# Linear attention and a 2:4-sparse feed-forward: the layer input of four tile pairs transposed by VectorE and HBM instead of TensorE

## The chip, the core and the metric

The kernel runs on one core of a Trainium2 chip, in float32 throughout. The metric is device time in microseconds. Five engines work side by side, each through its own queue of instructions in a fixed order: PE (TensorE, with its weight loads shown apart as PEld), DVE (VectorE), ACT (ScalarE), POOL (GpSimd) and SP, which here only issues DMAs. An instruction waits at the head of its queue for what it needs, and everything behind it waits too.

## What is computed

```python
# x: [2, 1024, 512]; 16 query heads, 4 key/value heads of 128
x = x + layernorm(attention(layernorm(x)))
x = x + layernorm(ffn(layernorm(x)))

# attention: q, k, v = x @ W.T; rope on q and k; elu + 1 on both;
#   state += k v^T and z += k along the sequence, out = (q state) / (q z + 1e-6); out @ Wo.T
# ffn: h = silu(x @ w_gate) * (x @ w_up); of each 4 neighbours the 2 largest are kept; h @ w_down
```

The change touches one thing in this: how the first `layernorm(x)` of half of the sequence gets from rows (tokens on partitions) into columns (model dimension on partitions), which is the form in which TensorE takes it as a factor.

## The kernel before

**Steps.** The attention part runs in 16 steps: eight chunks of 128 tokens (of both batch entries, a "tile pair") for the first half of the heads, and then the same eight for the second half (`STEPS = 2 * NC`). In step n TensorE makes the key/value and query products of tile pair n+1, the scores and attention of n, and the output products of n-1, woven by hand in the loop over `n`. Products are made by a seven-product scheme with sums of quarters, `chain` (L509). Its `snapshot` copies of a running bank, "u copies" below (L528, ACT), are waited for by the chain's next product into that bank.

**Input of a step.** In step n the pair n+2 is prepared. `step_normalize` (L672) takes statistics, root and normalization on DVE and ACT and leaves the result in `x`. Its root on ACT waits in the plan for the signal `("root", n)`, given after a step's fourth product. `step_input` (L680) is called late in the step, once for each of the two batch entries: four TensorE transposes into a PSUM bank (`transposed`, whose instructions carry L498), ACT copies out of it (L691, L697) and, for the second entry, four subtractions on DVE (L700, L704). This gives `xf`, seven factors of 128 x 256. They are stored to HBM (L707), and steps 8 to 15 read them from there (`step_input_again`, L713). In steps 6 and 7 the pairs n+2 are already these stored ones.

**A transpose without TensorE.** Queries and attention outputs go another way, `moved` (L625): DVE transposes 32x32 blocks within each partition group (L630) into one of three `blocks` buffers, one DMA stores the 256 KB to HBM (L636), and four DMAs of 64 KB read them back with blocks exchanged (L643).

**The order.** Nothing but TensorE's order is written by hand. The class `Plan` plays the engines through while the program is being built: each piece of work is a generator that yields (engine, length, rank) or a name to wait for, and of the work that is ready the lowest rank goes first. The rank is 1 unless given. What comes out is the fixed order of each queue. Lengths and transfer times in it are estimates, and a float that is yielded alone is a pause. Weights are prepared beside all this by `prepare_all`: loads on SP (L425), sums on POOL (L449), stores (L451), in parts that TensorE's progress sets free.

Other names used below: `features` (rope and elu+1 of queries and keys, with ACT lines 779 and 781), `attend` (the division is L972), `o_sums` (L1038, sums for the output products), `finish` (from step 8 on, layer norm of the attention output), `load` (of `x` at L311).

Of the kernel before, what the change touches and what calls it, by code (L numbers as in the profile page):

```python
# [10 lines left out]
F32 = mybir.dt.float32  # L11
BF16 = mybir.dt.bfloat16
AF = mybir.ActivationFunctionType
ALU = mybir.AluOpType
PSUM = bass.MemoryType.PSUM

P = 128
B, S, DM = 2, 1024, 512
# [3 lines left out]
NIC = DM // P  # L22
NC = S // P
# [88 lines left out]
def kernel(  # L112
# [16 lines left out]
    nc = tc.nc  # L129
# [3 lines left out]
    dram = ctx.enter_context(tc.tile_pool(name="dram", bufs=1, space=bass.MemoryType.DRAM))  # L133
# [9 lines left out]
        out=causal,  # L143
        in_=causal,
# [16 lines left out]
    xf_dram = [dram.tile([P, 7, 2, P], F32, name=f"xf{c}") for c in range(NC)]  # L161

    qb_dram, ob_dram = (
        [[dram.tile([P, 4 * P], F32, name=f"{of}{k}{i}") for i in range(4)] for k in range(2)]
        for of in ("qb", "ob")
    )

    fb_dram = [dram.tile([P, 4 * P], F32, name=f"fb{tt}") for tt in range(4)]
    y_dram = [dram.tile([P, B, DM], F32, name=f"y{c}") for c in range(NC)]
    x2_dram = [dram.tile([P, B, DM], F32, name=f"x2_{c}") for c in range(NC)]  # L170

# [113 lines left out]
    def left(name, bufs, **more):  # L285
        return actx.enter_context(
            tc.tile_pool(name=name, bufs=bufs, reuse_waits="tile", **more)
        )
# [9 lines left out]
    qp = left("a_q", 2)  # L298
# [7 lines left out]
    ln = right("a_ln", 2)  # L306
# [52 lines left out]
    xt, rope_sb = {}, {}  # L359
# [9 lines left out]
    root = const.tile([P, 1], F32, name="root")  # L369
# [85 lines left out]
    plan = Plan()  # L455
# [17 lines left out]
    uses = {}  # L473
# [3 lines left out]
    def ring(name, bufs):  # L477

        k = uses.get(name, 0)
        uses[name] = k + 1  # L480
        return [(name, k - bufs)] if k >= bufs else [], (name, k)
# [126 lines left out]
    def all_of(count, name):  # L608


        def done():
            nonlocal count
            count -= 1
            if count == 0:
                plan.signal(name)

        return done
# [4 lines left out]

    def moved(src, through, new, name, *names):  # L625


        yield "dve", 0.8
        t = qp.tile([P, 4, 4, 32], F32, tag="blocks", name="blocks", bufs=3)
        nc.vector.transpose(  # L630
            out=t.rearrange("p b i r -> p i b r"),
            in_=src.rearrange("p i (b d) -> p i b d", d=32),
        )
        yield 0.2
        yield "sp", 0.44
        nc.sync.dma_start(out=through, in_=t.rearrange("p b i r -> p (b i r)"))  # L636
        yield plan.transfer(256)
        for n in names:
            yield n
        for b in range(4):  # L640
            yield "sp", 0.44
            t = t if b else new()
            nc.sync.dma_start(  # L643
                out=t[b * 32 : (b + 1) * 32],
                in_=through.rearrange("(u d) (b e) -> b d u e", u=4, b=4)[b],
            )
            landing = plan.transfer(64)
        yield landing + 1.5
        plan.signal(name)
# [20 lines left out]
    xf = {}  # L670

    def step_normalize(n, root=None, rank=1):  # L672
        yield "x", n
        scales = yield from layernorm_pair([xt[n][:, b, :] for b in range(B)], B, "a", root, rank)
        for b in range(B):
            yield "dve", 0.56, rank
            normalize(xt[n][:, b, :], xt[n][:, b, :], *scales[b])
            plan.signal(("xn", n, b))

    def step_input(n, b, kind):  # L680

        if b == 0:
            xf[n] = ln.tile([P, 7, 2, P], F32, tag="xf", name="xf")
        t = xf[n]
        pt, name = transposed(
            xt[n][:, b, :].rearrange("p (c d) -> p c d", c=NIC), kind, ("xn", n, b)
        )

        def first():
            yield "act", 0.65, 0  # L690
            nc.scalar.copy(t[:, 0:2].rearrange("p q k d -> p (q k) d"), pt)  # L691
            plan.signal(name)
            plan.signal(("xf0", n))

        def second():
            yield "act", 0.4, 0
            nc.scalar.copy(t[:, 2], pt[:, 2:4, :])  # L697
            yield "xf0", n
            yield "dve", 0.45, 0
            nc.vector.tensor_tensor(t[:, 3], pt[:, 0:2, :], t[:, 0], ALU.subtract)  # L700
            plan.signal(name)
            for to, i0, i1 in ((4, 2, 3), (5, 4, 0), (6, 1, 4)):
                yield "dve", 0.45, 0
                nc.vector.tensor_tensor(t[:, to], t[:, i0], t[:, i1], ALU.subtract)  # L704
            plan.signal(("xf", n))
            yield "sp", 0.44, 2
            nc.sync.dma_start(out=xf_dram[n], in_=t)  # L707
            plan.transfer(896)
            plan.signal(("xf stored", n))

        plan.spawn((first, second)[b]())

    def step_input_again(n):  # L713
        yield "out", n - 2, 0
# [75 lines left out]
    kf, kT, v1, qT = {}, {}, {}, {}  # L790
# [73 lines left out]
    def q_products(n):  # L864
        def place():
            return rawp.tile([P, REP, HD], F32, tag="raw", name="qraw", bufs=5)

        def feature(i, done=None):
            def new():
                qT[n, i] = qp.tile([P, 4, P], F32, tag="qT", name="qT", bufs=4)  # L870
                return qT[n, i]

            def go(src):
                f = yield from features(src, n, done, None, int(n + i > 0))
                plan.signal(("features", n, i))
                if (n, i) in BY_PE:
                    first_q[n, i] = f
                    return
                yield from moved(
                    f, qb_dram[n % 2][i], new, ("qT", n, i), *([("out", n - 1, i)] if n else [])  # L880
                )

            return go

        def q21(b, name):
            yield from feature(2, name)(b)

        return chain(
            ("q", n),
            [P, REP, HD],  # L890
            1.72,
            project(weights[n // NC][1], n),
            lambda i: [("xf", n), ("w", n // NC, 1, i)],
            (qp, "keep512", 2),
            (place, feature(0)),
            (place, feature(3)),
            (place, feature(1)),
            q21,
        )
# [138 lines left out]
    def o_sums(n):  # L1038
        for i in (3, 0, 1, 2):
            yield "of", n, i  # L1040
        if n > 0:
            yield "o", n - 1, 4
        engine = "pool" if n + 1 < STEPS else "dve"

        def t3():
            yield engine, 1.3 if engine == "pool" else 0.75
            eng = nc.gpsimd if engine == "pool" else nc.vector
            eng.tensor_tensor(factor(n, 6 - 1, 1), of[n, 4], of[n, 0], ALU.subtract)
            plan.signal(("of", n, 5))

        yield "dve", 0.8
        nc.vector.tensor_tensor(of[n, 3], of[n, 3], of[n, 0], ALU.subtract)
        plan.signal(("of", n, 3, "sum"))
        yield "dve", 0.8
        nc.vector.tensor_tensor(factor(n, 4, 1), of[n, 2], of[n, 3], ALU.subtract)
        plan.signal(("of", n, 4))
        plan.spawn(t3())
        yield "dve", 0.8
        nc.vector.tensor_tensor(factor(n, 6, 1), of[n, 1], of[n, 4], ALU.subtract)
        plan.signal(("of", n, 6))  # L1060
# [125 lines left out]
    def run(g, times):  # L1186
        for _ in range(times):
            next(g, None)
# [520 lines left out]
    with tc.manual_schedule(engines={E.PE, E.Pool, E.SP, E.DVE, E.Activation}):  # L1709
# [66 lines left out]
        for n in range(STEPS):  # L1776
# [19 lines left out]
                plan.spawn(load(n + 3, "x"))  # L1796
            if n + 2 < STEPS:
                if n + 2 < NC:
                    plan.spawn(step_normalize(n + 2, ("root", n)))
                else:  # L1800
                    plan.spawn(step_input_again(n + 2))
            if n + 2 == NC:
# [45 lines left out]
            if n == 0:  # L1848
                q_transposed(0, 2)
                outputs(1)  # L1850
                run(kvp, 1)
                run(qpr, 1)
                q_transposed(0, 3)
                run(kvp, 1)
                step_input(2, 0, "a")
                outputs(2)
                step_input(2, 1, "a")
                run(qpr, 1)
                outputs(3)
            else:  # L1860
                outputs(1)
                run(qpr, 1)
                run(kvp, 1)
                run(qpr, 1)
                run(kvp, 1)
                run(opr, 2)
                outputs(2)
                if n + 2 < NC:
                    step_input(n + 2, 0, "a")
                run(opr, 2)  # L1870
            if n + 2 == STEPS:
                plan.need(("prepared",), *(("features", n + 1, i) for i in range(4)))
# [2 lines left out]
            if n > 0:  # L1875
                k_transposed(n + 1)
                run(opr, 1)
                if n + 2 < NC:
                    step_input(n + 2, 1, "a")
                outputs(3)  # L1880


# [114 lines left out]
```

## Time and profile before

| what | value |
|---|---|
| median of 3 runs | 1293.47 us (1291.8 to 1295.14) |
| the profiled run | 1293.64 us |
| its span on the core | 1291.9 us |
| four TensorE transposes of `x`, start to start | 0.43 us |
| TensorE transposes of `x` (L498) | 64 |
| DVE block transpose 128x512 (L630) | 0.66 to 0.715 us |
| ACT table load | 1.28 us |
| blocks read back (L643), issue to landing | 2.3 us median |

The span is measured inside the run, which is 1.7 us longer. In all views times are microseconds from the span's start unless ns is named. A row of the timeline has start, length, engine, line, operation, result <- operands, sizes and how many instructions in a row it merges; a bracket at the end is idle time before it and what ended it. A line of a source view has the operation and its count, then the shortest, median and longest duration in ns.

### The profile page before, as it was taken

What the parts mean: (1) busy time and instruction counts of PE and PEld (TensorE: products, weight loads), DVE (VectorE), ACT (ScalarE), POOL (GpSimd) and SP (SyncE); (2) the same over time, 40 slices, a digit from 0 to 9 for tenths busy, and PEclk for the clock granted to TensorE, in tenths of its full rate; (3) what the DMA queues carried; (4) which work ended last, traced back from release to release, by engine and by line L of the source; (5) the groups of instructions that cost most, each with busy time, mean ns of one, the idle gap of its engine ahead of it and who ended that gap; (6) DMA issues with size and microseconds to landing.
All of it is one profiled execution on the core that took longest, in us unless ns stands there. A gap on an engine that the chain in (4) does not pass through costs nothing. (4 is left out here: it accounts for less than half of the span.)

```text
span 1291.9 us, 17317 instructions
## 1 busy us (share of the span) xinstructions
PE 1265.8 (98%) x5868; PEld 1016.8 (79%) x5868; DVE 865.6 (67%) x1519; ACT 455.4 (35%) x905; POOL 340.8 (26%) x261
## 2 busy tenths in 40 slices
PE   7899999999999999999999999999999999999997
PEld 4567777777777777777788887888888888888886
DVE  6987877786666786678764487416981687426763
ACT  3644454444334344434443332113220333023211
POOL 4634442432232454455421101001100110110010
PEclk9999999999999999999999999999999999999999
DMA  7376668659757876676484498367547756465312
GB/s 249 118 244 199 199 231 278 206 194 312 221 195 210 289 228 230 221 236 204 160 249 155 136 265 235 99 199 217 154 123 228 236 155 196 148 189 174 108 44 87
DMA packets 280151, 252.57 MB, mean 196 GB/s; under 512 B 19200, under 2 KB 239104, under 8 KB 277376
## 3 DMA queue, kind: packets, MB, share of 16 engines
q1 hardware_dynamic: 278832, 249.64, 61.9%
q10 hardware_dynamic: 1232, 1.84, 0.4%
q8 instruction: 47, 0.77, 0.2%
q14 instruction: 40, 0.33, 0.1%
HBM read 179.83 MB, written 71.57 MB: 195 GB/s over the span
## 5 line engine op out<-in xcount | busy, mean ns | idle before, releaser
L528 ACT COPY u<-cb 128x512 f32<-128x512 f32 (+1 forms) x252 | 126.4, 503 | 492.5 <-PE cb L250 189.9
L736 PE MATMUL cb<-wq,xf 128*128 128x512 f32 x256 | 120.4, 593 | 1.3 <-ACT u L528 1.3
L1078 PE MATMUL cb<-wo,of 128*128 128x256 f32 x512 | 121.2, 380 | 0.0
L250 PE MATMUL cb<-fxnT,wgu 128*128 128x256 f32 x512 | 117.3, 379 | 2.4 <-issue 1.2
L250 PE MATMUL cb<-fxt,wgu 128*128 128x256 f32 x512 | 117.1, 380 | 1.4 <-ACT u L528 1.4
L776 POOL TENSOR_TENSOR qraw<-qraw,r 128x512 f32<-128x512 f32 x48 | 61.7, 1285 | 201.5 <-DVE qraw L767 174.9
L1078 PEld LDWEIGHTS cb<-wo,of 128*128 128x128 f32 x512 | 95.7, 190 | 23.1 <-issue 11.6
L972 ACT ACTIVATE o<-nm,den 128x128 f32<-128x128 f32 x256 | 73.8, 370 | 109.0 <-DVE state L995 84.2
L250 PEld LDWEIGHTS cb<-fxnT,wgu 128*128 128x128 f32 x512 | 97.1, 190 | 16.1 <-issue 3.1
L250 PEld LDWEIGHTS cb<-fxt,wgu 128*128 128x128 f32 x512 | 97.2, 190 | 15.3 <-ACT u L528 2.2
L1507 POOL TENSOR_TENSOR h<-h 128x512 f32<-128x512 f32 x16 | 26.1, 1629 | 286.9 <-DVE ht L1504 185.5
L539 DVE TENSOR_TENSOR y<-u,ce 128x256 f32<-128x256 f32 (+1 forms) x42 | 18.9, 452 | 117.3 <-ACT u L528 57.3
L449 POOL TENSOR_TENSOR wraw<-wraw 128x512 f32<-128x512 f32 x68 | 96.7, 1422 | 3.0 <-DMA of<-ob 0.4
L955 PE MATMUL nm<-v,am 128*128 128x129 f32 x512 | 96.1, 277 | 1.0 <-ACT o L972 1.0
L954 PE MATMUL nm<-state,qT 128*128 128x129 f32 x448 | 87.6, 278 | 0.0
L736 PEld LDWEIGHTS cb<-wq,xf 128*128 128x128 f32 x256 | 48.3, 190 | 47.7 <-issue 44.5
L955 PEld LDWEIGHTS nm<-v,am 128*128 128x128 f32 x512 | 77.1, 194 | 2.0 <-ACT o L972 1.8
L736 PEld LDWEIGHTS cb<-wkv,xf 128*128 128x128 f32 x256 | 49.1, 192 | 32.9 <-issue 27.3
L954 PEld LDWEIGHTS nm<-state,qT 128*128 128x128 f32 x448 | 72.5, 194 | 2.5
L736 PE MATMUL cb<-wkv,xf 128*128 128x256 f32 x256 | 66.8, 384 | 0.0
L910 PE MATMUL sc<-qT,kT 128*128 128x512 f32 x128 | 65.5, 593 | 0.0
L1078 PE MATMUL ce<-wo,of 128*128 128x256 f32 x256 | 60.5, 379 | 0.0
(172 smaller groups left out, 2458.1 us busy)
## 6 DMA issues: line engine op xcount, KB each, us to landing
wgu<-gs SPq DMA_DIRECT2D x64, 256.0 KB, 3.6
wgu<-us SPq DMA_DIRECT2D x64, 256.0 KB, 3.0
wd<-d_dram SPq DMA_DIRECT2D x32, 512.0 KB, 5.1
qb<-blocks SPq DMA_DIRECT2D x59, 256.0 KB, 2.3
qT<-qb SPq DMA_DIRECT2D x236, 64.0 KB, 2.3
ob<-blocks SPq DMA_DIRECT2D x58, 256.0 KB, 2.5
of<-ob SPq DMA_DIRECT2D x232, 64.0 KB, 2.3
xf<-xf SPq DMA_DIRECT2D x16, 896.0 KB, 4.7
```

Source lines behind the costliest of these rows:

```text
L250: nc.tensor.matmul(bank[:, j, :].rearrange("p (w t) -> p w t", t=32), w[:, k, j, :], xf[xi][:, k], start=(start and j == 0 and k == 0), st ...
L449: nc.gpsimd.tensor_tensor(to, i0, i1, op)
L528: nc.scalar.copy(kept[i], b)
L539: nc.vector.tensor_tensor(dst[:, rows], kept[i][:, rows], b, ALU.add)
L736: nc.tensor.matmul(bank.rearrange("p h d -> p (h d)"), xf[n][:, xi, k, :], w[wi][:, k, :], start=(start and k == 0), stop=(k == 1), skip_g ...
L776: nc.gpsimd.tensor_tensor(u, u, r, ALU.add)
L910: nc.tensor.matmul(sc.rearrange("p u h t -> p (u h t)"), kT[n][:, 2 * b + j, :], qT[n, i].rearrange("p u e -> p (u e)"), start=True, stop= ...
L954: nc.tensor.matmul(dst, q[:, u, :], state[b, j], start=True, stop=False)
L955: nc.tensor.matmul(dst, a[:, u, :], v, start=(c == 0), stop=True)
L972: nc.scalar.activation(t[:, u, :], nmv[:, u // 2, u % 2, 0:HD], AF.Copy, scale=den[:, u // 2, u % 2 : u % 2 + 1],)
L1078: nc.tensor.matmul(bank.rearrange("p h d -> p (h d)"), of[n, xi][:, k, :], weights[gp][2][wi][:, k, :], start=(start and k == 0), stop=(k ...
L1507: nc.gpsimd.tensor_tensor(b12, b22, b12, ALU.subtract)
```

## The change

Pairs 4 to 7 (prepared in steps 2 to 5) no longer call `step_input`. A new function, `step_input_moved`, is started at the beginning of their step: both entries pass through `moved`, with the last four sevenths of the `xf` tile as block buffers and the tile `x` itself as the place to read back to. After a pause of 5.0 in the plan ACT copies the factors from SBUF, and DVE makes the four subtractions from SBUF. Pairs 0 to 3 are transposed as before.

With it go three smaller edits: the root in `step_normalize` waits for no signal from step 1 on; `moved` waits in the plan until one of the three block buffers is free; and two output sums get rank 0 instead of 1.

```diff
@@ moved
-    def moved(src, through, new, name, *names):
-        yield "dve", 0.8
-        t = qp.tile([P, 4, 4, 32], F32, tag="blocks", name="blocks", bufs=3)
+    def moved(src, through, new, name, *names, blocks=None, rank=1):
+        k = -1
+        while not blocks and k < uses.get("blocks", 0) - 3:
+            k = uses["blocks"] - 3
+            yield "blocks", k
+        yield "dve", 0.8, rank
+        if not blocks:
+            block = ring("blocks", 3)[1]
+        t = blocks or qp.tile([P, 4, 4, 32], F32, tag="blocks", name="blocks", bufs=3)
...
         yield plan.transfer(256)
+        if not blocks:
+            plan.signal(block)
@@ new
+    def step_input_moved(n):
+        t = ln.tile([P, 7, 2, P], F32, tag="xf", name="xf")
+        xf[n] = t
+        both = all_of(2, ("xf0", n))
+
+        def tile_in(b):
+            yield "xn", n, b
+            x_ = xt[n][:, b, :]
+            to = x_.rearrange("p (u i r) -> p u (i r)", u=4, r=32)
+            yield from moved(
+                x_.rearrange("p (c d) -> p c d", c=NIC),
+                xb_dram[n % 2][b],
+                lambda: to,
+                ("xm", n, b),
+                blocks=t[:, 3 + 2 * b : 5 + 2 * b].rearrange(
+                    "p q k (i r) -> p (q k) i r", r=32
+                ),
+            )
+            yield 5.0
+            v = x_.rearrange("p (u i r) -> p i u r", u=4, r=32)
+            if b == 0:
+                yield "act", 0.65
+                nc.scalar.copy(t[:, 0:2].rearrange("p q k (u r) -> p (q k) u r", r=32), v)
+            else:
+                yield "act", 0.4
+                nc.scalar.copy(t[:, 2].rearrange("p k (u r) -> p k u r", r=32), v[:, 2:4])
+            both()
+            if b == 1:
+                yield "xf0", n
+                yield "dve", 0.45
+                nc.vector.tensor_tensor(
+                    t[:, 3].rearrange("p k (u r) -> p k u r", r=32),
+                    v[:, 0:2],
+                    t[:, 0].rearrange("p k (u r) -> p k u r", r=32),
+                    ALU.subtract,
+                )
+                for to_, i0, i1 in ((4, 2, 3), (5, 4, 0), (6, 1, 4)):
+                    yield "dve", 0.45
+                    nc.vector.tensor_tensor(t[:, to_], t[:, i0], t[:, i1], ALU.subtract)
+                plan.signal(("xf", n))
+                yield "sp", 0.44, 2
+                nc.sync.dma_start(out=xf_dram[n], in_=t)
...
+        for b in range(B):
+            plan.spawn(tile_in(b))
@@ o_sums, twice
-        yield "dve", 0.8
+        yield "dve", 0.8, 0
@@ loop over steps
-                    plan.spawn(step_normalize(n + 2, ("root", n)))
+                    plan.spawn(step_normalize(n + 2, None if n > 0 else ("root", n)))
+                    if n > 1:
+                        step_input_moved(n + 2)
...
-                if n + 2 < NC:
-                    step_input(n + 2, 0, "a")
+                if n == 1:
+                    step_input(3, 0, "a")
...
-                if n + 2 < NC:
-                    step_input(n + 2, 1, "a")
+                if n == 1:
+                    step_input(3, 1, "a")
```

More of the change, by code (lines that the diff above doesn't have):

```diff
@@ L168 @@
     fb_dram = [dram.tile([P, 4 * P], F32, name=f"fb{tt}") for tt in range(4)]
+    xb_dram = [[dram.tile([P, 4 * P], F32, name=f"xb{k}{b}") for b in range(B)] for k in range(2)]
     y_dram = [dram.tile([P, B, DM], F32, name=f"y{c}") for c in range(NC)]
@@ L711, in step_input @@
         plan.spawn((first, second)[b]())
+    def step_input_moved(n):
[39 more added lines that the diff above has]
+                nc.sync.dma_start(out=xf_dram[n], in_=t)
+                plan.transfer(896)
+                plan.signal(("xf stored", n))
+        for b in range(B):
+            plan.spawn(tile_in(b))
     def step_input_again(n):
@@ L879, in go @@
                 yield from moved(
-                    f, qb_dram[n % 2][i], new, ("qT", n, i), *([("out", n - 1, i)] if n else [])
+                    f,
+                    qb_dram[n % 2][i],
+                    new,
+                    ("qT", n, i),
+                    *([("out", n - 1, i)] if n else []),
+                    rank=1,
                 )
@@ L1049, in t3 @@
             plan.signal(("of", n, 5))
-        yield "dve", 0.8
+        yield "dve", 0.8, 0
         nc.vector.tensor_tensor(of[n, 3], of[n, 3], of[n, 0], ALU.subtract)
         plan.signal(("of", n, 3, "sum"))
-        yield "dve", 0.8
+        yield "dve", 0.8, 0
         nc.vector.tensor_tensor(factor(n, 4, 1), of[n, 2], of[n, 3], ALU.subtract)
```

## The prediction

> **What bounds the kernel now.** I read the page's first two parts, then a table of windows cut at the step borders, then TensorE's timeline, and last the waits. The page's chain of waits does not help: it goes back 2 us from the last output and stops.
>
> ```profile
> span 1291.9 us, 17317 instructions
> ...
> PE 1265.8 (98%) x5868; PEld 1016.8 (79%) x5868; DVE 865.6 (67%) x1519; ACT 455.4 (35%) x905; POOL 340.8 (26%) x261
> ...
> PE   7899999999999999999999999999999999999997
> ```
>
> TensorE is busy for 98% of the span, so only its own work and its few gaps can move the end. The next view cuts the attention part where a step's first query product starts (steps 2 to 6). Columns: window, its length, busy time of each engine, granted clock, DMA share, GB/s.
>
> ```profile
> 114.76:157.70 42.94, 42.94 (x206) 32.03 (x204) 34.04 (x62) 19.40 (x43) 20.22 (x15) 1.00 0.73 235
> 157.70:200.65 42.95, 42.95 (x206) 31.95 (x205) 32.45 (x63) 19.29 (x43) 17.69 (x13) 1.00 0.72 238
> 200.65:243.83 43.18, 43.17 (x205) 32.05 (x204) 33.79 (x63) 19.20 (x43) 16.33 (x13) 1.00 0.65 207
> 243.83:286.77 42.94, 42.94 (x205) 32.03 (x204) 33.61 (x58) 19.53 (x43) 16.76 (x13) 1.00 0.68 229
> 286.77:328.83 42.06, 42.06 (x197) 31.25 (x196) 25.72 (x51) 15.91 (x38) 8.91 (x7) 1.00 0.90 282
> ```
>
> The first four rows are the steps whose input (tile pairs 4 to 7) the change reroutes. TensorE has no gap in them, while DVE, ACT and POOL have 9 to 26 us to spare. The fifth row is nearly the after state: step 6 has the same products and attention, but its input comes ready from HBM. It has 8 matmuls fewer and is 0.88 us shorter. The timeline shows the pieces:
>
> ```profile
> 187.82 0.60 PE L498 MATMUL ca<-ident,x 128*128 128x128 f32 x4
> 188.25 1.89 PE L1078 MATMUL cb<-wo,of 128*128 128x256 f32 x8
> ...
> 193.87 0.61 PE L498 MATMUL ca<-ident,x 128*128 128x128 f32 x4
> ```
>
> Start to start, a group of four transposes holds TensorE for 0.43 us.
>
> **What the change removes.** Eight such groups, two in each of steps 2 to 5: 8 x 0.44 = 3.5 us. By whole steps it is 0.88 + 0.89 + 1.12 + 0.88 = 3.77 us, but 0.24 of step 4's 1.12 is a gap near 235 us, at a product after the key transposes; I don't count on it. **Sum: -3.5 us.** No part was hidden, since the removed instructions stood in a row without gaps.
>
> The skill speaks against this change: "VectorE: DVE Perf Modes", "Rules for kernel authors", says to transpose 128x128 on TensorE if PSUM will do. By it the detour loses, since DVE needs 0.70 us (rows at L630, 0.66 to 0.715) plus two transfers for what TensorE does in 0.43 us. The trace decides for the engine that is full: 0.43 us on the path against 0.70 us on an engine with 9 us free per step. The same page ("The three transpose paths") warns that a plain DMA which transposes by strides is 19 times slower than the crossbar; 19 times its 1309 ns gives an estimate of 25 us per 128x128 block, which would be late in every step. But the nearest row, the same reads for queries and outputs, shows runs of 512 bytes and a short landing:
>
> ```profile
> L643 SPq DMA_DIRECT2D qT<-qb x236: 302/430/2327, 60.4 to 662.2; - x118
> ...
> DMA to landing us min/median/max: 1.8/2.3/7.9
> ```
>
> So I take 2.3 us.
>
> **What it adds, per step.** DVE: two transposes, 1.4 us on 32 to 34 of 43. ACT: the same two copies, now from SBUF in runs of 32; not shown, bounded by 0.59 (L691) and 0.63 (L779, SBUF to SBUF), so at most 0.1 us more on an engine with 23 us free. DMA: 2 x 0.5 MB on 39 MB in the four steps, a tenth more; the share goes from about 0.70 to 0.77, under step 6's 0.90, which ran without a TensorE gap. SP: ten issues of 0.43 us, 4.3 us.
>
> **Is the input in time?** Statistics of tile pair n+2 are ready at about the step's start (bn_aggr at 157.1 for the step from 157.7). Without its gate the square root can go into ACT's hole before the first u copy (2.76 to 3.07 us in these steps; table load and root take 1.57). It now stands at 121.58, 164.51, 207.46 and 250.65, where nobody waits for it. Should it start late in the hole, it pushes the u copy of 159.62 by at most 1.57 us; that copy ends at 160.2 and the product that needs it starts at 161.99, 1.8 us later: cost 0. Normalizing (1.0) and two transposes (1.4) fit DVE's hole of 3.95 us. Then, from about 4 us into the step: store 2.3, eight issues 3.5, landing 2.3, so landed at some 13 us; the planner has 5.0 us in hand before it puts the copies in ACT's order, some 18 us into the step. SP can eat this: a weight load (L425) waits for its buffer in the queue until 125.17, 6.5 us, and all issues behind it wait too. Then the tile lands at about 19 us, and ACT waits 1 us for it. Behind the copy in ACT stand output divisions and u copies; at that place TensorE needs the next u copy 2.9 us or more after its end (copy ended 130.46, product at 133.40). So cost 0, up to some 3 us of lateness. The whole input is needed only at the next step's start, 25 us later.
>
> The four subtractions move from the step's dense end (DVE busy 12.04 of 13 us from 143 to 156) to its middle; there they free 1.7 us. The first one now has two SBUF operands. The skill ("SBUF - State Buffer", "SBUF: two separate sides") has such a DVE operation wait for a whole GpSimd one that reads SBUF, and the reverse. By it each could wait out a 1.3 to 1.6 us addition, four times: 6 us. The trace shows both:
>
> ```profile
> L704 DVE TENSOR_TENSOR xf<-xf x24: 411/424/1480, 10.3 to 282.9; 128x256 f32<-128x256 f32 x24
> ```
>
> Median 0.424, and up to 1.48 us beside POOL's additions at 152 to 155. I take 0.5 us each, with 1.1 us more for one of them: about 3 us on DVE between 18 and 25 us into the step, ahead of nothing that TensorE needs within 3 us. Cost 0; up to 1 us per step if an attention mask queues behind them.
>
> **Order edits.** The two output sums at rank 0 pass other DVE work of 0.7 us each: 0. The count of block buffers replaces real waits (DVE at L630 for a store: 3.9 us in all) by planned ones. What it could delay is a step's last query transpose. Its reads in step 3 were issued until 206.8 and landed at about 208.9; the scores that use them ran at 209.53, a slack of 0.6 us; in the steps beside it 4.2 and 6.3. Bounds: nothing gained, and at worst one store's landing (2.5 us) less 0.6, so 1.9 us in one step. I take 0, since DVE waited there already (0.57 us at 195.01).
>
> **Against which number.** The profiled run is 1293.64 us with a span of 1291.9; the runs' median is 1293.47. 1293.64 - 3.5 = 1290.1, and 1293.47 - 3.5 = **1290.0 us**. A change of 0.3%, 3.9 us, is about what a measurement of this kernel can tell from none. The forecast lies just inside.
>
> **Rivals.**
> - *More than the transposes goes.* Planned order shifts also in step 1, where TensorE waited 1.94 us for an ACT copy that stood behind an activation waiting for POOL, and then ran at half clock for 3.4 us (the matmuls from 76.86 stand 0.43 us per pair apart instead of 0.22, 1.6 us). For: the square root there loses its gate too. Against: its statistics end at 75.93, after that copy, so the order around it should stand. Worth 1.94 + 1.6, with step 4's gap: 1290.0 - 3.8 = 1286.2.
> - *Partly given back.* A query transpose lands late through SP's longer queue: 1 to 2 us in one to three of the steps, so 1291 to 1295. For: the slack of 0.6 us. Against: SP's added issues lie in the first half of a step, and the 896 KB store of the factors leaves its busy end.
> - *Slower.* The input's reads stand behind SP's blocked weight load, and ACT's copy waits for them with the u copies behind it. It costs nothing until the lateness passes 2.9 us. At 6 us (the blocked 6.5 us on top of a full queue) it is 3.1 us per step, 12.4 in four, so 1302; at 5 us, 1298. It decides from 3.8 us of lateness, where the 0.88 us of a step is used up. For: this wait is real in step 2. Against: in the next three it is 2.3 to 3.5 us.
> - *It does not do what it says:* transposes of pairs 4 to 7 still on TensorE. The call sites exclude it.
>
> **How the numbers follow.** Forecast 0.56, spread by about 1 us of measurement and small order effects: 0.24 of it lies beyond 0.3%, 0.32 within. More than the transposes 0.09, all faster. Partly given back 0.14, within. Slower 0.21. So faster 0.33, within 0.46, slower 0.21. The range goes from 1288 to 1297: the forecast with its spread, the given-back case and the mild end of the slower one; it leaves out most of the first and the bad end of the slower rival. Within the forecast alone it is 1289 to 1291.
>
> **What would show it.** Right: steps 2 to 5 of about 42.06 us each with TensorE busy throughout, 32 transposes of x at L498 instead of 64, the square root in the hole at a step's start, x landed before ACT's copies, and steps 7 to 15 and the second half of the kernel as long as before. Wrong: a TensorE gap in these steps behind an ACT copy or a late query transpose, a granted clock below 1.00 after it, or an SP wait that pushes the reads of x past 20 us into the step.

## The result: 5 us slower, and where they are lost

| | before | after |
|---|---|---|
| median of 7 runs on the same chip | 1293.90 us (1291.80 to 1296.44) | 1298.88 us (1296.62 to 1302.27) |
| profiled run / its span | 1293.64 / 1291.9 us | 1298.88 / 1297.2 us |

The ratio after / before is 1.0041, with a 95% interval of 1.0027 to 1.0054. 1290.0 us were forecast, in a range of 1288 to 1297.

The page's first two parts, of the kernel after:

```profile
span 1297.2 us, 17296 instructions
...
PE 1264.0 (97%) x5836; PEld 1013.0 (78%) x5836; DVE 868.3 (67%) x1527; ACT 455.0 (35%) x905; POOL 338.8 (26%) x261
...
PE   7999999899999999999999999999999999999997
```

TensorE lost its 32 transposes (5868 to 5836 instructions) and is busy 1.8 us less, yet the span is 5.3 us longer. So TensorE is now idle for longer, and the eighth slice, at about 227 to 259 us, shows a digit 8 where the page of before had only nines.

To find the place, the first score product of each step (TensorE's order was not changed) is set against the same product of before. The table has the growth of this difference from step to step, in us, from the two timelines.

| step | 2 | 3 | 4 | 5 | 6 and 7 |
|---|---|---|---|---|---|
| after minus before | -0.87 | +0.66 | +0.10 | +4.98 | 0.00 |

A step goes here from its first score product to the next step's; the second of the four in step 5 begins at 257.27 us. Step 2 does what was forecast for each of the four. The other three do not, and in steps 6 and 7 nothing more is lost. TensorE's waits, of after (what was waited for, us in all, times, longest):

```profile
PE sc L974 <- DMA qT<-qb: 4.0, 1, 4.0
...
PE ca L500 <- DVE kf L843: 1.4, 1, 1.4
...
PE ce L1142 <- DVE y L541: 1.0, 1, 1.0
```

None of the three is in the list of before. TensorE's timeline shows them in place:

```profile
192.43 0.63 PE L500 MATMUL ca<-ident,kf 128*128 128x128 f32 x4 [1.37 <-DVE kf L843]
...
200.34 1.99 PE L1142 MATMUL ce<-wo,of 128*128 128x256 f32 x8 [0.96 <-DVE y L541]
...
257.27 2.04 PE L974 MATMUL sc<-qT,kT 128*128 128x512 f32 x2 [3.99 <-DMA qT<-qb]
259.11 1.75 PE L795 MATMUL cb<-wkv,xf 128*128 128x256 f32 x4
```

The bracket is the idle time before the instruction. After the longest gap the two score products take 2.04 us, where the same pair took 1.02 us before, and the four products behind them 1.75 instead of 1.03: TensorE runs at about half rate for a while (granted clock 0.66 in the window from 257 to 262 us). From the second to the third score product of step 5 it is 10.60 us instead of 8.89, so this costs 1.7 us.

The account of steps 2 to 5, by the distances of the score products: -0.88 x 4 = -3.52 for the transposes; +1.54 around the key gap, +1.23 around the `y` gap, +4.15 (queries) and +1.71 (half rate); -0.24 for a small gap of before in step 4 that is gone. That is the +4.87 to which the table sums. The rest of the span's 5.3 us was there already at step 2 (0.5 us).

**How the three gaps arise.** The DVE timeline of after, at the end of the step that leads to the longest gap:

```profile
235.91 1.08 DVE L754 TENSOR_TENSOR xf<-x,xf 128x256 f32<-128x256 f32 x1
237.02 3.13 DVE L762 TENSOR_TENSOR xf<-xf 128x256 f32<-128x256 f32 x3
...
240.78 0.71 DVE L638 STREAM_TRANSPOSE blocks<-qraw 128x512 f32<-128x512 f32 x1
...
243.97 0.70 DVE L638 STREAM_TRANSPOSE blocks<-qraw 128x512 f32<-128x512 f32 x1
```

and of before:

```profile
234.79 0.71 DVE L630 STREAM_TRANSPOSE blocks<-qraw 128x512 f32<-128x512 f32 x1
...
237.81 0.71 DVE L630 STREAM_TRANSPOSE blocks<-qraw 128x512 f32<-128x512 f32 x1
...
238.75 0.41 DVE L700 TENSOR_TENSOR xf<-ca,xf 128x256 f32<-128x256 f32 x1
239.20 1.22 DVE L704 TENSOR_TENSOR xf<-xf 128x256 f32<-128x256 f32 x3
```

The subtractions have changed places with the query transposes, and they take 4.2 us instead of 1.6. Both query transposes come about 6 us later. What that does is seen on SP, in the timeline of after:

```profile
241.52 0.32 SPq L644 DMA_DIRECT2D qb<-blocks  x1
...
245.26 0.43 SPq L453 DMA_DIRECT2D us<-wraw  x1
249.54 0.38 SPq L427 DMA_DIRECT2D wraw<-in_w_up_dram  x1
250.02 0.45 SPq L644 DMA_DIRECT2D qb<-blocks  x1
250.57 2.42 SPq L653 DMA_DIRECT2D qT<-qb  x4
...
257.62 2.90 SPq L653 DMA_DIRECT2D qT<-qb  x4
```

in SP's waits from 240 to 262 us, of after:

```profile
SPq L427 <- DMA us<-wraw: 3.8, 1, 3.8
```

and in SP's timeline of before:

```profile
238.97 1.82 SPq L643 DMA_DIRECT2D qT<-qb  x4
...
251.10 0.38 SPq L425 DMA_DIRECT2D wraw<-in_w_up_dram  x1
```

SP stands still from 245.7 to 249.5 us. Its next instruction is a weight load, and this waits until the store ahead of it has read the buffer. The score product at 257.27 needs the first of the two query blocks. Its store was issued at 241.52 and had landed at 244.8, but its reads stand behind the blocked load, and behind the second block's store at 250.02. They are those issued from 250.57 to 253. They run beside the megabyte just released and take 4.6 to 5.5 us to land, where the same reads took 2.0 to 2.1 us before: the last lands at 257.14. (The second block's reads follow at 257.62.) In the kernel before the first block's reads were issued from 238.97 on and had landed at 242.4, ahead of the weight load, which was blocked there too, 3.0 us, until 251.10.

The key gap is in step 3 and the `y` gap at the start of step 4. Ahead of the key gap, DVE stands still for 4.8 us (timeline of after):

```profile
180.75 0.69 DVE L1116 TENSOR_TENSOR of<-of 128x512 f32<-128x512 f32 x1 [4.83 <-DMA of<-ob]
...
191.00 1.29 DVE L843 SCALAR_TENSOR_TENSOR kf<-kraw,r 128x512 f32<-128x512 f32 x1
...
196.84 3.12 DVE L762 TENSOR_TENSOR xf<-xf 128x256 f32<-128x256 f32 x3
199.88 0.41 DVE L541 TENSOR_TENSOR y<-u,ce 128x256 f32<-128x256 f32 x1
```

An output sum waits for four reads that land 6.0 us (median) after their issue, beside a weight load and the two new stores of `x`. DVE works off its backlog with hardly a pause and makes `kf` at 191.00, 2.9 us later than before. The `y` gap is plainer: `y` stands directly behind three subtractions that take 3.12 us, ends at 200.29, and TensorE goes on at 200.34.

### The profile page after: what moved, and what is told of

It is laid out like the page before. It is cut to its first block, busy times and chain, and to the rows that moved or that the text cites. A ratio compares the mean times of both kernels' runs of the same rounds, so it can differ in the third digit from the quotient of the medians.

```text
span 1297.2 us, 17296 instructions
## 1 busy us (share of the span) xinstructions
PE 1264.0 (97%) x5836; PEld 1013.0 (78%) x5836; DVE 868.3 (67%) x1527; ACT 455.0 (35%) x905; POOL 338.8 (26%) x261
## 3 DMA queue, kind: packets, MB, share of 16 engines
q1 hardware_dynamic: 284592, 253.83, 62.3%
## 5 line engine op out<-in xcount | busy, mean ns | idle before, releaser
L835 POOL TENSOR_TENSOR qraw<-qraw,r 128x512 f32<-128x512 f32 x48 | 61.8, 1288 | 194.3 <-DVE qraw L826 163.0
```

The source lines that it names most:

```text
L835: nc.gpsimd.tensor_tensor(u, u, r, ALU.add)
```

## The experiments

An edit to the planned work makes the planner lay out the queues anew, so it can move more than one thing. Two groups of kernels are exceptions, as a comparison of the orders in the traces shows. Leaving out POOL's weight sums left the orders of DVE, ACT and SP as they were. And "without the count" has in every queue the order of after, "without both" that of "without rank 0": each pair is one program profiled twice, and shows how far two profiles of it differ (+4.87 and +6.24, +2.19 and -0.57 us below). The ratios are to the kernel before, measured on the same chip, with 95% intervals; "2 to 6" is the growth of TensorE's lag behind the profile of before from step 2's first score product to step 6's (after: +4.87), and "6 to 8" the same for the two next steps (after: 0.00).

| kernel | ratio (interval) | 2 to 6, us | 6 to 8, us |
|---|---|---|---|
| before + order edits | 1.0010 (0.9996 to 1.0024) | -0.03 | +0.87 |
| without the count | 1.0038 (1.0022 to 1.0055) | +6.24 | 0.00 |
| without rank 0 | 1.0049 (1.0032 to 1.0066) | +2.19 | +7.36 |
| without both | 1.0040 (1.0026 to 1.0054) | -0.57 | +7.02 |
| no subtractions | 1.0033 (1.0016 to 1.0050) | +1.21 | +1.35 |
| no detour through HBM | 1.0029 (1.0020 to 1.0039) | +2.81 | +2.12 |
| input at rank 0 | 1.0059 (1.0040 to 1.0078) | +1.82 | +3.05 |
| subtractions planned at 1.3 | 1.0057 (1.0037 to 1.0077) | +2.77 | +5.88 |
| subtractions on POOL | 0.9991 (0.9982 to 1.0000) | -0.41 | +1.37 |
| the same, without rank 0 | 0.9988 (0.9975 to 1.0000) | +0.01 | +1.75 |
| the same, with a pause | 0.9995 (0.9986 to 1.0003) | -2.99 | +1.67 |
| loads never blocked | 1.0020 (1.0009 to 1.0031) | -2.34 | +1.69 |
| before, loads never blocked | 1.0014 (1.0002 to 1.0026) | -0.26 | 0.00 |
| POOL and loads never blocked | 1.0068 (1.0050 to 1.0087) | +1.93 | +1.41 |
| no weight sums | 1.0015 (1.0004 to 1.0026) | +5.11 | +0.01 |
| before, no weight sums | 0.9959 (0.9945 to 0.9972) | -0.27 | +0.01 |
| one load later | 1.0023 (1.0013 to 1.0034) | +1.65 | +0.45 |
| one load later, no weight sums | 0.9990 (0.9982 to 0.9997) | +6.13 | 0.00 |

**The order edits alone and taken back.** First theory: the count of block buffers makes the query transposes late. The kernel before with the three order edits (count, rank 0, root without its signal):

```diff
+        while k < uses.get("blocks", 0) - 3:
+            k = uses["blocks"] - 3
+            yield "blocks", k
-        yield "dve", 0.8
+        yield "dve", 0.8, 0
-                    plan.spawn(step_normalize(n + 2, ("root", n)))
+                    plan.spawn(step_normalize(n + 2, None if n > 0 else ("root", n)))
```

> The kernel before with only the three order edits (count, rank 0, free square root). Order theory: slower than before by 3 to 8 us, since the gaps come with the edits. Contention or queue theory: as before within 1.5 us.

The kernel after without the count:

> The changed kernel without the count of the block buffers. Order theory (the count postpones a step's last query transposes, which then store behind SP's blocked weight load): the 4.0 us wait of the scores for qT and the half clock after it (1.7 us) go, so about 5.5 us less than the changed kernel, at or a little under before. Contention theory (the four subtractions, now with two SBUF operands, take 3.9 to 4.9 us beside POOL's weight sums where they took 1.6): the subtractions stay as long, and the time stays within 2 us of the changed kernel's.

Without rank 0 at the two output sums:

> The changed kernel with the two output sums back at rank 1. Order theory (at rank 0 the first sum stands early in DVE's queue and holds it until the outputs land, 12.4 us in four steps against 2.0 before): the waits at that line fall under 4 us, the 1.4 us gap before the key transposes goes, 1.5 to 3 us less than the changed kernel. Contention theory: within 2 us of the changed kernel.

Without both:

> The changed kernel without the count and without rank 0: the route through HBM and the freed square root alone. Order theory: what was forecast, 3.5 us under before. Contention or queue theory: still slower than before, by 2 to 6 us, with TensorE gaps in steps 3 to 5.

The edits alone cost nothing that can be told from none, and no gap opens in steps 2 to 5. Without the count the queues do not change, so the query gap stays (3.45 us), as do those of keys (1.38) and `y`: the count is not the cause.

Rank 0 has more to do with it. In both kernels without it step 5 has no query gap: the first query block is transposed ahead of the subtractions, and its reads go ahead of the weight load (SP's timeline of "without rank 0"):

```profile
247.85 1.81 SPq L653 DMA_DIRECT2D qT<-qb  x4
...
254.87 0.38 SPq L427 DMA_DIRECT2D wraw<-in_w_up_dram  x1
```

But DVE's waits at the output sums do not fall under 4 us, as was expected: they are 14.4 us in "without rank 0" (12.4 in after). The key and `y` gaps stay (1.3 to 1.7 us), and step 7 loses 4.9 us in the one and 4.3 us in the other. From the timelines of "without both", TensorE and then DVE:

```profile
330.88 3.53 PE L1139 MATMUL ce<-wo,of 128*128 128x256 f32 x8 [4.34 <-DVE y L541]
```

```profile
329.81 0.71 DVE L635 STREAM_TRANSPOSE blocks<-qraw 128x512 f32<-128x512 f32 x1 [7.52 <-DMA qb<-blocks]
```

DVE holds a transpose for 7.5 us until a block buffer's store has been done, with `y` behind it (8.25 us in "without rank 0"; 3.2 us in after). So rank 0 at the output sums takes part in where the loss falls, but without it another gap as long opens two steps later, and the time is no better.

**The subtractions and the detour.** The four subtractions left out, and, separately, the stores and reads of `x` left out:

```diff
-                yield "dve", 0.45
-                nc.vector.tensor_tensor(
...
-                for to_, i0, i1 in ((4, 2, 3), (5, 4, 0), (6, 1, 4)):
-                    yield "dve", 0.45
-                    nc.vector.tensor_tensor(t[:, to_], t[:, i0], t[:, i1], ALU.subtract)
```

> The changed kernel with the four subtractions of pairs 4 to 7 left out (four of the seven factors are not computed), so DVE loses 4 to 5 us in the busy end of each of steps 2 to 5. Contention theory: no TensorE gap of over 0.5 us in steps 2 to 5 and the forecast gain, about 3.5 us under before (8.5 to 9 under the changed kernel). Queue theory (ten more issues and 1 MB per step on SP make the reads of outputs and queries late): gaps at the scores and at the key transposes stay, at most 2 us less than the changed kernel.

> The changed kernel with the stores and reads of x left out (pairs 4 to 7 enter untransposed), its DVE transposes, copies and subtractions kept and planned at the same times. Queue theory: the gaps of steps 3 to 5 go, about 3.5 us under before. Contention theory: the subtractions still take about 1.4 us each of three, gaps at y and at the key transposes stay, 0 to 6 us over before.

Without the subtractions all three gaps are gone, but others of 0.4 to 1.6 us open in the same steps (`v`, `u`, an attention mask), and the time stays (1298.55 against 1298.88 us) where 8.5 to 9 us less were expected. Without the detour the subtractions still take 1.38 us each at the median, so it is not the transfers that slow them; DVE's waits at the output sums fall from 12.4 to 5.6 us. Neither part carries the loss alone.

How far the subtractions are stretched shows in the source view of `xf` on DVE, of after (count, then shortest, median and longest in ns):

```profile
L762 DVE TENSOR_TENSOR xf<-xf x12: 411/1374/1482, 150.4 to 286.8; 128x256 f32<-128x256 f32 x12
...
L754 DVE TENSOR_TENSOR xf<-x,xf x4: 747/752/1078, 149.7 to 284.3; 128x256 f32<-128x256 f32 x4
```

The same three subtractions had a median of 424 ns before. They stand 34 to 40 us into the step now, beside four weight sums that POOL runs without a pause, here at 148 to 154 us:

```profile
148.39 5.94 POOL L451 TENSOR_TENSOR wraw<-wraw 128x512 f32<-128x512 f32 x4
```

Three edits change their place or engine: rank 0 for copies and subtractions, 1.3 instead of 0.45 in the plan, or POOL:

```diff
-                    yield "dve", 0.45
-                    nc.vector.tensor_tensor(t[:, to_], t[:, i0], t[:, i1], ALU.subtract)
+                    yield "pool", 0.75
+                    nc.gpsimd.tensor_tensor(t[:, to_], t[:, i0], t[:, i1], ALU.subtract)
```

> The changed kernel with ACT's copies and the four subtractions at rank 0, so that they come some us earlier. Contention theory: if they then run before POOL's weight sums begin, they take 0.42 us each and the gaps shrink, 2 to 6 us less than the changed kernel; if they still meet POOL, no gain. Queue theory: within 2 us of the changed kernel.

> The changed kernel with the four subtractions planned at 1.3 instead of 0.45 each, nearer to what they take. If the planned order is wrong only because their length is: y and the transposes come ahead of some of them, the gap at y goes, 1 to 5 us under the changed kernel. If DVE simply lacks the time there: within 1.5 us of it.

> The changed kernel with the four subtractions on POOL instead of DVE. Contention theory: DVE is freed of 4 to 5 us in each step's busy end, the gaps at y and at the key transposes go, and the time is 2 to 4 us under before. Queue theory: stays within 2 us of the changed kernel, with the wait for qT.

At rank 0 the subtractions are fast again (median 425 ns), and planned at their real length the key gap shrinks to 0.3 us. Both kernels are slower all the same: 2.6 us for queries in the one, 1.9 us for `v` and 3.9 us for an ACT copy in step 7 in the other. On POOL the loss goes: 1293.05 us against 1293.79 of before. This has no three long operations ahead of the query transposes or `y`; four gaps of 0.5 to 1.1 us are left, some 3.0 of the 3.5 us saved. Two attempts at these, without rank 0 and with a pause of 3 us in the plan ahead of the output sums:

```diff
+        if n > 0:
+            yield 3.0
```

> Subtractions on POOL, output sums back at rank 1. If rank 0 is what puts the output sum early in DVE's queue: DVE's wait there falls from 16 us in steps 2 to 6 to under 6, and 1 to 2.5 us under the version with the subtractions on POOL. If the reads are late in any order: within 1 us of it.

> Subtractions on POOL, and 3 us of pause in the plan after the output reads, ahead of the output sums. If the rest of the gain is lost because the plan takes the reads for landed when they are not: DVE's wait at the output sum falls under 5 us, the gaps of 0.5 to 1.1 us go, and the time is 2.5 to 4 us under before. If not: within 1 us of the version without the pause.

With the pause DVE's waits for output reads go from 7.1 to 4.1 us (steps 2 to 5) and nearly the whole saving shows up at step 6, 2.99 us. Then an ACT copy in step 7 and a later query cost 2.8 us, and the medians say 1293.58 against 1293.87. None of the three is faster than before by more than 0.3%; the best stands 0.12% below it, and its interval reaches 1.

**The blocked load.** A pause behind each weight store, so that in the plan no load is issued before its buffer is free; in the kernel after, with POOL besides, and in the kernel before:

```diff
             nc.sync.dma_start(out=dst, in_=q)
-            plan.transfer(1024)
+            yield plan.transfer(1024) + 2.5
```

> The changed kernel, with a pause in the plan after each store of a prepared weight block, so that the next weight load enters SP's queue only when its buffer is about to be free and does not block the queue. If the blocked weight load turns DVE's lateness into the late query transpose: SP's waits at the weight load go from over 20 us in steps 2 to 5 to under 5, the 4.0 us wait for qT and its half clock go, and the time is 4 to 6 us under the changed kernel; the 1.4 and 1.0 us gaps (key transposes, y) stay unless they too came through SP. If contention alone matters: within 2 us of the changed kernel.

> Subtractions on POOL and weight loads that do not block SP, both. If these two causes are what ate the gain: no TensorE gap over 0.5 us in steps 2 to 6 and 2.5 to 3.5 us under before. If something else holds output reads back: 0 to 1.5 us under before, as with the subtractions on POOL alone.

> Control: the kernel before with the same pause after each store of a prepared weight block. TensorE has no gap there in steps 2 to 5, so nothing to gain: as before within 1 us.

After this edit step 5 has no query gap, and one of 0.64 us (keys) is all that is left in steps 2 to 5: 2.34 us saved there. Behind step 6 a `y` and a query gap of 1.4 us each eat most of it. Its median is 3.2 us under that of after, less than the 4 to 6 expected. Against its own control it is 1295.65 to 1295.39: no difference (the control itself is 1.5 us over before, where under 1 was expected). But the edit shifted POOL too (the subtractions were back at 424 ns), so it does not tell the load from the contention. With POOL it missed: 1301.45 us.

**Contention taken away.** POOL's weight sums left out, in after and in before:

```diff
-                nc.gpsimd.tensor_tensor(to, i0, i1, op)
```

> The changed kernel with the weight sums on POOL left out of the preparation (the prepared weights are then only copies), with their loads, stores and planned times kept, so SP blocks as before and POOL leaves the SBUF alone. Contention theory: the subtractions fall to 0.42 us each, the gaps at y, at the key transposes and the 4.0 us at the scores go, 2.5 to 4 us under its control. Queue theory: the subtractions are short too, but the scores still wait 2 us or more for qT, and the time is over its control.

> Control: the kernel before with the same weight sums left out. TensorE had no gap to lose there: as before within 1.5 us.

In the source view of this kernel, and in TensorE's timeline:

```profile
L761 DVE TENSOR_TENSOR xf<-xf x12: 418/424/426, 146.5 to 282.2; 128x256 f32<-128x256 f32 x12
```

```profile
252.97 2.05 PE L973 MATMUL sc<-qT,kT 128*128 128x512 f32 x2 [4.05 <-DMA qT<-qb]
```

All twelve subtractions are fast, so POOL's sums are what stretches them. The `y` gap is gone and the key gap is 0.16 us. The query gap is there in full. Against its control (before, without the sums) both query transposes are late, the first at 234.64 us on DVE instead of 229.78: the subtractions stand ahead of them, short as they are. The reads of the first block are again behind the blocked weight load:

```profile
245.27 0.38 SPq L427 DMA_DIRECT2D wraw<-in_w_up_dram  x1
245.75 0.45 SPq L643 DMA_DIRECT2D qb<-blocks  x1
246.29 2.42 SPq L652 DMA_DIRECT2D qT<-qb  x4
```

In the control they were issued at 232.84. So contention costs the two small gaps, and the order on DVE and SP the large one. Against its control, 1290.12 us, this kernel is 5.85 us slower: contention is not the main part. (The control was expected within 1.5 us of before and is 3.75 us under it by the medians, 0.41% by the ratio.)

**One load, eight microseconds later.** The edit that moves one position in a queue: the weight load that SP was blocked at.

```diff
             if n + 1 < len(units):
+                if n + 1 == 8:
+                    yield 8.0
                 loaded = yield from load_unit(n + 1)
```

> The changed kernel with one weight load (the one that blocked SP from 245.7 to 249.5) 8 us later in the plan; SP's queue differs in the places of that load, of the x stores and reads of step 5 beside it, and DVE in a few neighbours. Queue theory: the wait of the scores for qT in step 5 falls from 4.0 to under 0.5 us and the clock stays at full speed, 5 to 6 us under the changed kernel, so about as before (within 1.5 us); the gaps of 1.4 us (key transposes) and 1.0 us (y) in step 3 stay as they are. Otherwise: within 2 us of the changed kernel.

Up to 249 us the orders on SP and DVE are those of after. Then, in SP's timeline of this kernel:

```profile
245.46 0.44 SPq L455 DMA_DIRECT2D us<-wraw  x1
246.00 0.39 SPq L646 DMA_DIRECT2D qb<-blocks  x1
246.49 3.68 SPq L655 DMA_DIRECT2D qT<-qb  x4
...
256.09 0.43 SPq L427 DMA_DIRECT2D wraw<-in_w_up_dram  x1
```

The reads of the first query block are issued from 246.49 instead of 250.57; the score product at 253.83 waits for nothing and runs at full rate. Step 5 goes from +4.98 to +0.13 us. The medians say 1296.11 against 1298.88, by their ratios 1.0023 (1.0013 to 1.0034) and 1.0041 (1.0027 to 1.0054), measured on different chips and overlapping a little. That is 2.8 us where 5 to 6 were expected. The key and `y` gaps stay, 1.38 and 0.95 us. A new one of 1.35 us (a `u` copy at 188.05) came although the order ahead of it is unchanged: the output reads landed later in this run (median 6.5 us after issue instead of 6.0), and DVE stood 6.46 us at the output sum instead of 4.83. It is no work of the edit: the second profile of after's program ("without the count") has it too, 1.59 us, behind a wait of 7.3 us.

**Both taken away.** The late load and no weight sums:

> The same move of one weight load, with POOL's weight sums left out. If the queue's block and the contention are the two causes: no TensorE gap over 1.5 us in steps 2 to 6, and 5 to 6 us under the run without POOL's sums, so within 1.5 us of its control or under it (the forecast gain of 3.5 less the gap of 1.3 that it had at an ACT copy). If something else is lost in this route: 2 us or more over the control.

No query gap, fast subtractions, and yet +6.13 us in steps 2 to 5. 1292.14 us stand against 1290.12 of the control (on different chips; by the ratios to before, 0.9990 and 0.9959), although 3.5 us of transposes are gone. Where it goes now is in DVE's waits (steps 2 to 5):

```profile
DVE of L1117 <- DMA of<-ob: 17.2, 3, 9.3
DVE blocks L639 <- DMA qb<-blocks: 4.6, 3, 3.2
```

and in TensorE's gaps behind them:

```profile
183.01 0.49 PE L1020 MATMUL nm<-v,am 128*128 128x129 f32 x2 [2.29 <-DVE am L987]
...
266.70 3.50 PE L796 MATMUL ce<-wq,xf 128*128 128x512 f32 x4 [2.38 <-DVE qraw L542]
```

A third loss, then: output sums at the head of DVE's queue wait up to 9.3 us for their reads, and an attention mask and a query sum stand behind them. In the kernel before the same wait comes to 2.0 us in all, in that after to 12.4 (DVE's waits in steps 2 to 5, after and then before):

```profile
DVE of L1116 <- DMA of<-ob: 12.4, 4, 4.8
```

```profile
DVE of L1052 <- DMA of<-ob: 2.0, 1, 2.0
```

## Why the prediction was wrong

*What is removed: right.* Each step without a gap is 0.87 to 0.89 us shorter: step 2 of after, and in kernels where step 4's or 5's gaps are gone those as well. 32 instructions fewer, 3.5 us. The Trainium skill's rule ("VectorE: DVE Perf Modes", "Rules for kernel authors": transpose 128x128 on TensorE if PSUM will do) would have been right about the outcome. But the prediction weighed it by DVE's 0.70 us, and it was not these that cost here, but the orders and the contention that came with the detour.

*Is the input in time: right in effect, off in its times.* The root went into ACT's hole and nobody waited for it. The reads of `x` were issued 17 to 21 us into the step, not from some 6 on, and ACT's copies ran at 22 to 31 us, not 18. No TensorE gap stands behind them. The "slower" rival named the right sign and the right obstacle, the blocked load, but behind it stood queries and not the input, and ACT was not what waited.

*What is added: here it failed.* "About 3 us on DVE between 18 and 25 us into the step, ahead of nothing that TensorE needs within 3 us. Cost 0" is the step that was wrong, in place and in size:

- In place: the subtractions stood at 34 to 40 us, in the dense end, ahead of query transposes and `y`. The prediction took the 5.0 us of the planner's margin as the end of the delay, and did not ask what the rank-1 queue on DVE and SP puts in between.
- In size: 3.9 to 4.9 us per step, not 3. The Trainium skill ("SBUF - State Buffer", "SBUF: two separate sides") has such a DVE operation and a GpSimd one wait for each other in full, and by it the prediction had an estimate of 6 us; I took 0.5 us each with one exception. The trace agrees in kind: beside POOL's sums 0.75 and three times 1.37 us at the median, without these sums 0.38 and 0.42. The trace of before had shown 1.48 us as the longest; with POOL's sums back to back, that row was near the median to take. With these sums left out the two gaps of 1.4 and 1.0 us fall to 0.16 and 0.

*"Partly given back": right in kind, wrong in step and price.* It was a query transpose that landed late. I placed it where the slack was least, 0.6 us, and priced it at 1 to 2 us; it came in step 5 and cost 4.15 + 1.7. The slack was misread too. The reads issued until 206.8 are those of the step's last block, which the product at 229.91 waits for; the product at 209.53 uses the four ahead of them (SP's timeline of before):

```profile
198.57 3.20 SPq L643 DMA_DIRECT2D qT<-qb  x4
...
204.97 1.82 SPq L643 DMA_DIRECT2D qT<-qb  x4
```

These four had landed at 204.3, so the slack there was 5.2 us, and in step 5, where I had read 6.3, it was 10.3 (landed at 242.4, used at 252.72). Even that did not help, for the slack was read as time and it was a position: the reads were ahead of a load blocked for 3.0 us. Once the transposes were some 6 us later on DVE, the first block's reads fell behind that load. This added its wait, slower transfers beside the released megabyte, and TensorE's half rate. One load moved takes 4.85 us of the step away. The rival was capped at one store's landing because only the count was asked for what delays the store, and the runs clear the count.

*Order edits at 0: right for themselves.* On the kernel before they show 1.0010 (0.9996 to 1.0024). Together with the new traffic this 0 does not hold: without rank 0 the query transpose stays ahead of the subtractions, and step 5 has no query gap. And "pass other DVE work of 0.7 us each: 0" left out that the sum, put first, then waits for its reads with all of DVE behind it: 12.4 us in steps 2 to 5 of after, 2.0 before. But without rank 0 these waits were 14.4 us. With the stores and reads of `x` left out they were 5.6 us, which points to reads that land late behind and beside `x`'s transfers; since the orders changed there too, no run isolates it. Waits and stretched operations both have a part in the gaps: with the same order and nearly the same wait (6.46 us in "one load later", 6.39 in "no weight sums") the key gap is 1.38 us beside POOL's sums and 0.16 without them, while the gap at the `u` copy is 1.35 and 1.27 us in the two, and none in the profile of after, whose wait was 4.83.

## What to carry to other kernels

Slack read off a timeline holds only as long as the order in the queues stays: before moving work on an engine with time to spare, look at which DMA it hands to the issuing queue, and what that queue is blocked by a few positions further on. An operation's duration is to be taken from rows with the neighbours that it will have; here the same subtraction is 0.42 us alone and 1.37 us beside GpSimd's sums. And when a planner lays out all queues, a saving of 0.3% on the full engine is smaller than what one changed position can be worth: here 3.5 us against 4.85. A planner that knows nothing of a wait, here for the weight buffer, will put reads behind it. Giving it that wait was not enough here: with loads never blocked the kernel was level with its control, and no version collected the saving.

## What was not expected of the hardware

- TensorE's half rate after a gap came in the middle of a stage in which it was otherwise full: after a gap of 3.99 us the score pair took 2.04 instead of 1.02 us and 1.7 us were lost. In steps 1 to 8 of all the profiles here, each of the five gaps of 3.9 us and more (3.92, 3.99, 4.05, 4.34, 4.89) was followed within 2 us by a granted clock of about a half. Of the gaps between 1.9 and 3.5 us some were (1.94, 2.29, 2.38) and some were not (2.44, 2.57, 3.45), so no limit can be read from these. The 3.45 us were the query gap in the second profile of after's program: whether the 1.7 us come on top can differ from one execution to the next.
- Without POOL's weight sums the kernel before became 0.41% faster (0.28 to 0.55%), mostly in step 1: the gap in front of a key/value product falls from 1.94 to 0.85 us, and the half rate that followed it is gone.
- The same order of instructions does not give the same gaps: with output reads landing at 6.5 instead of 6.0 us, one wait on DVE grew from 4.83 to 6.46 us and a gap of 1.35 us opened. Two profiles of one program differed by up to 2.8 us in steps 2 to 5.
